# Perceiver block on one core: most transposes of the feed-forward's activations go from the matrix engine to VectorE squares and an exchange through DRAM

## The chip, the cores and the metric

One Trainium2 chip, of which one core is used. The metric is the device time of one execution in microseconds (us), lower is better. The engines of the core are named as in the profile: PE (TensorE, matrix products; PEld is its weight load), DVE (VectorE), ACT (ScalarE), POOL (GpSimd), SP (SyncE, which here only issues DMAs).

## The reference

A perceiver block in float32: cross-attention of 16 x 64 latents to 16 contexts of 512 rows, a differential self-attention, and a feed-forward with blockwise FP4 rounding. Each is added to the residual `x`. Only the feed-forward is touched by the change:

```python
x = x + _L0_xattn_ref(ctx_1024, _layernorm(x), ...)        # 16 batches x 64 latents, width 512
x = x + _L0_attn_ref(_layernorm(x), ...)
x = x + _L0_ffn_ref(_layernorm(x), w_gate, w_up, w_down)   # hidden width 1408

def fp4_quant_dequant(x):          # blocks of 16 along the last axis
    scale = max(|block|) / 6       # at least 1e-12
    return nearest of {0, .5, 1, 1.5, 2, 3, 4, 6} to |x| / scale, times sign(x) * scale

def fp4_linear(x, w):
    return einsum('bsk,nk->bsn', fp4_quant_dequant(x), fp4_quant_dequant(w))

def ffn(x):
    h = silu(fp4_linear(x, w_gate)) * fp4_linear(x, w_up)
    return fp4_linear(h, w_down)
```

## The kernel before

The 1,024 latent rows are eight tiles of 128 rows (`t` = 0 to 7). The kernel runs the latents' projections, cross-attention, self-attention and the feed-forward one after the other; the start of the feed-forward is woven into the end of self-attention. The order that each engine follows up to there is written out by hand and pinned by `in_order()`. What `FeedForward.rest` issues after that is put in order, engine by engine, by the framework's own planner, which works with a simulated timeline; the engines then run their queues strictly in that order and meet through semaphores.

Every float32 product is made of three products of rounded halves: an operand `a` is split into `hi`, a copy in the reduced format fp32r, and `lo = a - hi`, and `terms` (L114) runs hi by hi, hi by lo and lo by hi. So the first operand's upper half is needed for the first two thirds of a product and its lower half for the last third.

The feed-forward is a list of 24 steps `(t, c)`, where `c` is a chunk of the hidden width: 512, 512 and 384 columns. The list starts (0,0), (0,1), (1,0), (1,1), (0,2), (1,2), and goes on tile by tile with (2,0), (2,1), (2,2) up to (7,2). Step `n` (`step`, L1820) issues:

- `gate` and `up` of step n: 12 matmuls each, left operand the transposed activations `x` of the tile (`fx`, both halves), into a pair of PSUM banks `gu` of which there are two;
- between them `turn_h` of step n-2: three or four PE transposes of 128 x 128 (`ht`, L171) into PSUM, the upper half copied by ACT (`hh`, L129), the lower half subtracted by DVE (`hl`, L130; it reads `ht` in PSUM and `hh` in SBUF);
- `hidden` of step n: ACT's silu of the gate bank (L1744), DVE's product with the up bank (L1745), and the FP4 rounding of `h` (`fp4_steps`, L194 to L210). All of the rounding is on DVE but one ACT operation in the middle (L205), which stands between DVE's L202 and L207;
- `down` of step n-3: 12 or 9 matmuls on `hh` and `hl`; after chunk 2 DVE adds the residual (L1797) and SP stores the tile `y`;
- where a tile's turn has come, `norm` of a later tile (layer norm and FP4 rounding of x in `fz`; here the two broadcast products L199 and L210 are POOL's), and `turn` (four PE transposes `xt`, ACT's copy, DVE's subtraction `fx`).

Of the kernel before, what the change touches and what calls it, by code (L numbers as in the profile page):

```python
# [9 lines left out]
F32 = mybir.dt.float32  # L10
F32R = mybir.dt.float32r
# [3 lines left out]
ALU = mybir.AluOpType  # L15
# [4 lines left out]
P = 128  # L20
D = 512
KC = D // P
# [7 lines left out]
CHUNKS = [(at, min(D, FF - at)) for at in range(0, FF, D)]  # L30
# [15 lines left out]
def f32(t):  # L46

    return t.bitcast(F32)


class Common:
# [7 lines left out]
    def __init__(self, ctx, tc):  # L59
        nc = tc.nc  # L60
        self.tc, self.nc = tc, nc
        const = ctx.enter_context(tc.tile_pool(name="const", bufs=1))
        self.const = const
        self.ident = const.tile([P, P], F32, tag="ident", name="ident")
        make_identity(nc, self.ident)
        self.mhalf = const.tile([P, 8], F32, tag="mhalf", name="mhalf")
        nc.gpsimd.memset(self.mhalf, -0.5)
        self.mmagic = const.tile([P, 1], F32, tag="mmagic", name="mmagic")
        nc.gpsimd.memset(self.mmagic, -MAGIC)
        self.masked = const.tile([P, 1], F32, tag="masked", name="masked")  # L70
        nc.gpsimd.memset(self.masked, -MASKED)
        self.rsw, self.rsT = (const.tile([P, 32], F32, tag=n, name=n) for n in ("rsw", "rsT"))
        nc.gpsimd.memset(self.rsw, 0.0)
        self.x_mv = const.tile([P, NT, 3], F32, tag="x_mv", name="x_mv")
        self.x = [const.tile([P, D], F32, tag=f"x{t}", name=f"x{t}") for t in range(NT)]
        self.small = ctx.enter_context(tc.tile_pool(name="small", bufs=4))
        self.slots = ctx.enter_context(tc.tile_pool(name="slots", bufs=1))
        self.ps_mm = ctx.enter_context(tc.tile_pool(name="ps_mm", bufs=3, space=PSUM))
        self.ps_sim = ctx.enter_context(tc.tile_pool(name="ps_sim", bufs=2, space=PSUM))
        self.ps_av = ctx.enter_context(tc.tile_pool(name="ps_av", bufs=1, space=PSUM))  # L80
# [137 lines left out]
class Scratch:  # L218


    def __init__(self, ctx, tc):
        pool = ctx.enter_context(tc.tile_pool(name="scratch", bufs=1, space=DRAM))

        def dram(name, shape):
            return pool.tile(shape, F32, tag=name, name=name)


        self.q = [dram(f"q_d{g}", [P, KC, GT * P]) for g in range(NT // GT)]
        self.k = [dram(f"k_d{g}", [P, KC, GT * P]) for g in range(NT // GT)]
        self.v = [dram(f"v_d{p}", [P, D]) for p in range(NT)]  # L230
        self.rs = [dram(f"rs_d{b}", [1, N]) for b in range(B)]

        self.gu = {
            (w, c): dram(f"{w}_d{c}", [P, 2, KC, n])
            for w in ("g", "u")
            for c, (_, n) in enumerate(CHUNKS)
        }
        self.dn = [dram(f"d_d{c}", [P, 2, n // P, D]) for c, (_, n) in enumerate(CHUNKS)]


class Quantise:
# [129 lines left out]
class CrossWeights:  # L371
# [20 lines left out]
    def turn(self):  # L392
        cm, nc = self.cm, self.cm.nc
        n = len(self.NAMES) * KC
        pt = cm.tr("vec_t")[:, :n]
        nc.tensor.transpose(pt, self.rows, cm.ident[:n, :n])
        nc.scalar.copy(self.vec, pt)
# [73 lines left out]
def _latents(ctx, tc, cm, sc, i, cw, cx, sa):  # L471
# [373 lines left out]
    def turned(*tiles):  # L845
        for p in tiles:
            turn(p)
            upper(p)
            lower(p)
# [10 lines left out]
def cross_attention(tc, cm, sc, i, cw, cx, w1, w2, att, quant):  # L860
# [276 lines left out]
    for b in range(B):  # L1137
# [16 lines left out]
        if b:  # L1154
            turn(b - 1)
            turn_latents(b - 1)
# [88 lines left out]
        quant.tick()  # L1245
        cx.load(b + 3)
    turn(B - 1)
    turn_latents(B - 1)
    att.product(0, "Wq")
# [35 lines left out]
def by_half(t):  # L1285

    return t.rearrange("p (c h) d -> p h c d", h=2)


class SelfAttention:  # L1290
# [199 lines left out]
    def squares(self, t):  # L1490
        o = self.st["o", t] = self.w1.tile([P, 8, S], F32, tag="oh", name=f"on_{t}")
        for h, po in enumerate(self.st["po", t]):
            self.nc.scalar.activation(by_half(o)[:, h], po, AF.Square)
# [146 lines left out]
class FeedForward:  # L1640


    def __init__(self, tc, cm, sc, w1, w2, out):
        self.tc, self.cm, self.nc, self.sc, self.out = tc, cm, tc.nc, sc, out
        self.w1, self.w2 = w1, w2
        self.W, self.st = {}, {}

        self.steps = [(t, c) for t in range(2) for c in range(2)] + [(t, 2) for t in range(2)]
        self.steps += [(t, c) for t in range(2, NT) for c in range(len(CHUNKS))]

    def weights(self, *names):

        at = {
            ("g", 0): (4, 5),
            ("u", 0): (10, 11),
            ("d", 0): (6, 7),
            ("g", 1): (0, 1),  # L1660
            ("u", 1): (8, 9),
            ("d", 1): (4 * ["prT"], ["o", "o", "q_hl"]),
            ("g", 2): (["four1", "four2"], 4 * ["v"]),
            ("u", 2): (2, 3),
            ("d", 2): (["pr", "oh"], ["pr", "q_e"]),
        }
        bufs = {"prT": 4, "v": 4, "o": 2, "pr": 2}
        for w, c in names:
            src = self.sc.dn[c] if w == "d" else self.sc.gu[w, c]
            _, _, nk, n = src.shape  # L1670
            for h, home in enumerate(at[w, c]):
                chunks = self.W[w, c, h] = []
                if isinstance(home, int):
                    pieces = [(self.cm.slot(home, f"{w}T{c}{h}", F32R, (P, nk, n)), nk)]
                else:
                    pieces = []
                    for x, tag in enumerate(home):
                        many = 2 if tag in ("four1", "four2", "q_hl", "pr") else 1
                        t = self.w1.tile(
                            [P, many, n], F32R, tag=tag, bufs=bufs.get(tag, 1), name=f"{w}T{c}{h}_{x}"  # L1680
                        )
                        pieces.append((t, many))
                for t, many in pieces:
                    k = len(chunks)
                    self.nc.sync.dma_start(f32(t), src[:, h, k : k + many])
                    chunks += [t[:, x, :] for x in range(many)]

    def norm(self, t):
        for step in self.norm_steps(t):
            step()  # L1690

    def norm_steps(self, t):
# [11 lines left out]

        return [begin, norm] + 5 * [lambda: next(st["fp4", t])]

    def turn(self, t):
        cm, w2 = self.cm, self.w2
        pt = cm.ps_av.tile([P, D], F32, tag="av", name=f"xt_{t}") if t < 2 else cm.tr(f"xt_{t}")
        cm.transpose_chunks(pt, self.st.pop(("z", t)), KC)  # L1710
        both = w2.tile([P, 2, KC, P], F32R, tag=f"fx{t % 2}", name=f"fx_{t}")
        cm.split(both[:, 0], both[:, 1], pt.rearrange("p (k n) -> p k n", n=P))
        self.st["x", t] = both[:, 0], both[:, 1]
# [38 lines left out]
    def turn_h(self, s):  # L1752
        cm, w2 = self.cm, self.w2
        t, c = s
        n = CHUNKS[c][1]
        nk = n // P
        pt = cm.tr(f"ht_{t}_{c}")
        cm.transpose_chunks(pt, self.st.pop(("h", s)), nk)
        hh = w2.tile([P, KC, P], F32R, tag="two_h", bufs=2, name=f"hh_{t}_{c}")[:, :nk, :]
        hl = w2.tile([P, KC, P], F32R, tag="two_l", bufs=2, name=f"hl_{t}_{c}")[:, :nk, :]  # L1760
        src = pt[:, :n].rearrange("p (k n) -> p k n", n=P)
        if s == self.steps[-1]:
            for k in range(nk):
                cm.nc.scalar.copy(hh[:, k, :], src[:, k, :])
            cm.nc.vector.tensor_tensor(hl, src, f32(hh), ALU.subtract)
        else:
            cm.split(hh, hl, src)
        self.st["hT", s] = hh, hl

    def down(self, s):  # L1770
        cm, nc = self.cm, self.nc
# [48 lines left out]
    def step(self, n):  # L1820
        s = self.steps[n] if n < len(self.steps) else None
        if s:
            self.gate(s)
        if 0 <= n - 2 < len(self.steps):
            self.turn_h(self.steps[n - 2])
        if s:
            self.up(s)
            self.hidden(s)
            if s[1] == 2 and 2 <= s[0] < NT - 2:
                self.norm(s[0] + 2)  # L1830
            elif s in ((1, 1), (0, 2)):
                self.norm(1 + s[1])
        if 0 <= n - 3:
            self.down(self.steps[n - 3])
        if s and (s == (1, 2) or (s[1] == 1 and 2 <= s[0] < NT - 1)):
            self.turn(s[0] + 1)
# [103 lines left out]
```

## Time and profile before

| | |
|---|---|
| time, median of 3 runs | 882.5 us (882.25 to 883.4) |
| the profiled execution: its own time, its span | 882.59 us, 880.8 us |
| busy, share of the span: PE, DVE, ACT, POOL | 99%, 78%, 45%, 35% |
| granted PE clock | 1.00 |
| PE transposes `ht`, in groups of 3 or 4 | 88, from 696.2 to 874.3 us |
| PE transposes `xt` | 32, from 667.2 to 837.4 us |
| first `gu` matmuls of chunk 2 of tile 3, 4, 5, 6, 7 | 764.85, 789.15, 813.48, 837.80, 861.69 us |
| DMA share of the 16 engines, 716 to 862 us | 0.01 to 0.06 |

The page gives one execution. A row of the timeline has the start in us, the duration in us, the engine, the source line, the operation, the tiles written and read, the shape and the count; brackets at its end give the engine's idle time before it and what ended it. Successive DVE operations can overlap by some hundredths of a microsecond, so their pace is read from start to start. The table of stretches gives the busy time of PE, PEld, DVE, ACT and POOL in each stretch, then the PE clock, the DMA share and GB/s.

### The profile page before, as it was taken

The numbers are of one execution on the slowest core, as the hardware profiler recorded it, in microseconds if no ns is written. First come the engines' busy times: TensorE is split into PE (matmuls) and PEld (weight loads), VectorE is DVE, ScalarE is ACT, GpSimd is POOL, SyncE is SP. The second block draws the span as 40 slices with busy tenths as digits, with TensorE's granted clock in tenths as the row PEclk, the third lists the DMA queues.
The fourth block names the chain that finished last, engine by engine and source line by source line (L and its number), as shares of the span: only waits on it lengthen the run. The fifth ranks groups of instructions, "written<-read, shape, count | busy, mean of one in ns | idle before, by whom it ended". The sixth has DMA issues, their size and how long they took to land.

```text
span 880.8 us, 17489 instructions
## 1 busy us (share of the span) xinstructions
PE 873.1 (99%) x6743; PEld 719.2 (82%) x6743; DVE 685.2 (78%) x1425; ACT 398.2 (45%) x787; POOL 305.3 (35%) x357
## 2 busy tenths in 40 slices
PE   8999999999999999999999999999999999999998
PEld 8988777877787888778877887888888888888887
DVE  7734457788788786787878866588998897888876
ACT  5653454544554535354436455555555233332221
POOL 2344334335353352352543622545543120111100
PEclk9999999999999999999999999999999999999999
DMA  8464554644555455435644361240007330000000
GB/s 295 148 234 171 163 163 143 201 144 146 187 175 154 142 163 167 135 112 179 185 131 146 123 197 56 91 192 2 1 3 312 143 144 13 13 13 13 12 13 25
DMA packets 80379, 111.12 MB, mean 126 GB/s; under 512 B 33176, under 2 KB 39080, under 8 KB 79016
## 3 DMA queue, kind: packets, MB, share of 16 engines
q1 hardware_dynamic: 80136, 109.48, 37.9%
q8 instruction: 53, 0.87, 0.4%
q0 software_dynamic: 160, 0.52, 0.2%
q14 instruction: 30, 0.25, 0.1%
HBM read 84.26 MB, written 25.72 MB: 125 GB/s over the span
## 4 chain that ended last, share of the span: by engine, by line
PE 94%; DVE 4%; POOL 1%; issue 0%; ACT 0%; DMA 0%; DVEq 0%; ACTq 0%; POOLq 0%
PE pv L121 20%; PE pk L121 20%; PE gu L121 14%; PE dn L121 7%; PE av L1043 5%; PE sim L971 4%; PE lv L121 2%; PE po L121 2%; PE Wv L121 2%; PE wo L121 2%; PE prt L1008 2%; PE Wq L121 2%; PE lq L121 2%; PE lk L121 2%; PE Wk L121 2%; PE ht L171 1%
## 5 line engine op out<-in xcount | busy, mean ns | idle before, releaser
L121 PE MATMUL pv<-xvh,x 128*128 128x512 f32 x512 | 132.7, 393 | 0.0
L121 PE MATMUL pk<-x,xkh 128*128 128x512 f32 x512 | 128.2, 392 | 0.0
L121 PEld LDWEIGHTS pv<-xvh,x 128*128 128x128 f32 x512 | 94.8, 188 | 26.0 <-issue 7.0
L121 PEld LDWEIGHTS pk<-x,xkh 128*128 128x128 f32 x512 | 94.9, 188 | 19.5 <-issue 0.4
L994 ACT ACTIVATE pr<-pr,least 128x576 f32<-128x576 f32 x64 | 49.2, 770 | 60.8 <-DVE least L990 60.8
L945 DVE TENSOR_TENSOR k<-pk,row 128x512 f32<-128x512 f32 x64 | 43.2, 675 | 40.2 <-PE pk L121 39.4
L368 POOL TENSOR_TENSOR x<-raw,x 128x512 fp32r<-128x512 f32 x32 | 41.3, 1289 | 84.6 <-ACT x L362 73.0
L958 ACT ACTIVATE v<-pv,rs 128x512 f32<-128x512 f32 x64 | 43.2, 684 | 59.8 <-PE pv L121 59.6
L121 PE MATMUL pv<-xvl,x 128*128 128x512 f32 x256 | 68.5, 389 | 0.0
L121 PE MATMUL pk<-x,xkl 128*128 128x512 f32 x256 | 68.5, 389 | 0.0
L121 PE MATMUL gu<-uT,fx 128*128 128x512 f32 (+1 forms) x288 | 66.7, 377 | 0.0
L121 PE MATMUL gu<-gT,fx 128*128 128x512 f32 (+1 forms) x288 | 65.8, 376 | 0.0
L121 PEld LDWEIGHTS gu<-gT,fx 128*128 128x128 f32 x288 | 52.2, 188 | 7.6 <-ACT fx L129 0.2
L121 PEld LDWEIGHTS gu<-uT,fx 128*128 128x128 f32 x288 | 51.9, 188 | 7.2
L121 PEld LDWEIGHTS pv<-xvl,x 128*128 128x128 f32 x256 | 48.0, 188 | 10.2
L121 PEld LDWEIGHTS pk<-x,xkl 128*128 128x128 f32 x256 | 48.0, 188 | 10.1
L990 DVE CUSTOM_DVE_ANT_0 pr<-sim,mask 128x576 f32<-128x576 f32 x64 | 45.9, 754 | 6.9 <-PE sim L971 6.6
L205 ACT ACTIVATE qe_h<-qe_h,mmagic 128x512 f32<-128x512 f32 (+1 forms) x24 | 16.5, 688 | 66.4 <-DVE qe_h L202 64.3
L321 DVE BATCH_NORM_STATS2 cst<-nat 128x6 f32<-128x512 f32 x64 | 42.8, 669 | 3.6 <-DMA nat<-in_ctx_dram 3.6
L121 PE MATMUL dn<-dT,hh 128*128 128x512 f32 x170 | 42.9, 392 | 0.0
L1043 PEld LDWEIGHTS av<-v,prT 128*64 128x64 f32 x1024 | 36.7, 138 | 6.9 <-issue 5.7
L1043 PE MATMUL av<-v,prT 128*64 128x64 f32 x1024 | 40.8, 224 | 0.0
(348 smaller groups left out, 1906.6 us busy)
## 6 DMA issues: line engine op xcount, KB each, us to landing
nat<-in_ctx_dram SPq DMA_DIRECT2D x16, 1024.0 KB
raw<-in_ctxT_dram SPq DMA_DIRECT2D x64, 256.0 KB
d_d<-qhl_d SPq DMA_DIRECT2D x11, 512.0 KB
row<-rs_d SPq DMA_DIRECT2D x16, 256.0 KB
g_d<-qhl_g SPq DMA_DIRECT2D x8, 512.0 KB
u_d<-qhl_u SPq DMA_DIRECT2D x8, 512.0 KB
gT<-g_d SPq DMA_DIRECT2D x4, 1024.0 KB
uT<-u_d SPq DMA_DIRECT2D x4, 1024.0 KB
```

The costliest lines, as they stand in the source:

```text
L121: self.nc.tensor.matmul(ps, lhsT=p[i], rhs=p[j], start=start and n == 0, stop=stop and n == last)
L171: self.nc.tensor.transpose(pt[:, c * P : (c + 1) * P], src[:, c * P : (c + 1) * P], self.ident)
L205: nc.scalar.activation(e, e, AF.Relu, bias=self.mmagic, scale=MAGIC)
L321: nc.vector.bn_stats(st, self.nat[b][:, j, :])
L368: by.tensor_tensor(lo, self.raw[:, c, :], f32(hi), ALU.subtract)
L945: nc.vector.tensor_tensor(k[:, S : S + N], ps, cx.row[b], ALU.mult)
L958: nc.scalar.mul(v, ps, cx.rs[b][:, t : t + 1])
L971: nc.tensor.matmul(pss[r][c * S : (c + 1) * S, h, :half], lhsT=queries[b % 2][rows, m, :], rhs=st["k"][m][rows, at : at + half], start=Tru ...
L990: nc.vector.tensor_tensor_reduce(two(pr), ps[:, :, :half], two(mask), -1.0, BIG, ALU.add, ALU.min, least)
L994: nc.scalar.activation(pr, pr, AF.Exp, bias=least, scale=-1.0, accum_out=st["tot"][:, t : t + 1])
L1008: nc.tensor.transpose(pt[:, c, at : at + S], state[b]["pr", a][rows, r, first + j * P : first + (j + 1) * P], cm.ident[rows, rows],)
L1043: nc.tensor.matmul(st["av"][rows, 2 * a + r, :], lhsT=w[:, rows], rhs=v[:, at : at + S], start=(n == 0), stop=(n == len(pairs) - 1),)
```

## The change

Two kinds of transposes leave PE: those of x for the tiles 2 to 7, and those of h for the steps (1,1) to (7,0) of the list, 19 of 24. In their place:

- `squares`: one DVE transpose of 32 x 32 squares (all squares of a tile in one instruction, the four groups of 32 columns brought forward as the outer index), then four DMAs on SP, one for each group of 32 partitions, that write 512-byte (or 384-byte) runs to a DRAM buffer `sq`, of which there are four;
- `regroup`: one DMA on SP that reads the buffer back with the groups exchanged (`raw`), ACT's copy of the upper half from `raw`, and POOL's subtraction of the lower half.

`send` and `send_h` issue the first part right after the rounding, `turn` and `turn_h` the second at their old place in the step. The SBUF tiles `k0`, `k1`, `k2` and `four0`, used by the attention before, hold the squares and `raw`, two each in turn. x of the tiles 0 and 1, h of the first three steps and of the last two keep PE, and there the lower half stays with DVE.

```diff
@@ Scratch
+        self.sq = [dram(f"sq_d{n}", [4, 32, 4, KC * 32]) for n in range(4)]
@@ FeedForward.__init__
+        self.far = self.near = 0
+        self.far_steps = self.steps[3:-2]
@@ FeedForward
+    def squares(self, src, nk, name):
+        nc = self.nc
+        tag = ("k0", "k1")[self.far % 2]
+        t = self.w1.tile([P, 4, KC * 32], F32, tag=tag, name=f"sq_{name}")[:, :, : nk * 32]
+        nc.vector.transpose(
+            t.rearrange("p q (k l) -> p q k l", l=32),
+            src.rearrange("p (k q l) -> p q k l", q=4, l=32),
+        )
+        far = self.sc.sq[self.far % len(self.sc.sq)][:, :, :, : nk * 32]
+        self.far += 1
+        for n in range(4):
+            nc.sync.dma_start(far[:, :, n].rearrange("q f r -> f q r"), t[n * 32 : (n + 1) * 32])
+        return far
+
+    def regroup(self, hi, lo, far, nk, name):
+        nc = self.nc
+        pool, tag = ((self.w1, "k2"), (self.w2, "four0"))[self.near % 2]
+        self.near += 1
+        raw = pool.tile([P, 4, KC * 32], F32, tag=tag, name=f"sr_{name}")[:, :, : nk * 32]
+        nc.sync.dma_start(raw, far.rearrange("q f t r -> (q f) t r"))
+        src = raw.rearrange("p t (k l) -> p k t l", l=32)
+        hi, lo = (x.rearrange("p k (t l) -> p k t l", l=32) for x in (hi, lo))
+        nc.scalar.copy(hi, src)
+        nc.gpsimd.tensor_tensor(lo, src, f32(hi), ALU.subtract)
+
+    def send(self, t):
+        if t >= 2:
+            self.st["zs", t] = self.squares(self.st.pop(("z", t)), KC, f"x_{t}")
+
+    def send_h(self, s):
+        if s in self.far_steps:
+            self.st["hs", s] = self.squares(self.st.pop(("h", s)), CHUNKS[s[1]][1] // P, f"h_{s[0]}_{s[1]}")
@@ turn
-        pt = cm.ps_av.tile([P, D], F32, tag="av", name=f"xt_{t}") if t < 2 else cm.tr(f"xt_{t}")
+        if t >= 2:
+            both = w2.tile([P, 2, KC, P], F32R, tag=f"fx{t % 2}", name=f"fx_{t}")
+            self.regroup(both[:, 0], both[:, 1], self.st.pop(("zs", t)), KC, f"x_{t}")
+            self.st["x", t] = both[:, 0], both[:, 1]
+            return
+        pt = cm.ps_av.tile([P, D], F32, tag="av", name=f"xt_{t}")
@@ turn_h
+        if s in self.far_steps:
+            self.regroup(hh, hl, self.st.pop(("hs", s)), nk, f"h_{t}_{c}")
+            return
         pt = cm.tr(f"ht_{t}_{c}")
         cm.transpose_chunks(pt, self.st.pop(("h", s)), nk)
@@ step
             self.hidden(s)
+            self.send_h(s)
             if s[1] == 2 and 2 <= s[0] < NT - 2:
                 self.norm(s[0] + 2)
+                self.send(s[0] + 2)
             elif s in ((1, 1), (0, 2)):
                 self.norm(1 + s[1])
+                self.send(1 + s[1])
```

More of the change, by code (lines that the diff above doesn't have):

```diff
@@ L1756, in turn_h @@
         nk = n // P
+        hh = w2.tile([P, KC, P], F32R, tag="two_h", bufs=2, name=f"hh_{t}_{c}")[:, :nk, :]
+        hl = w2.tile([P, KC, P], F32R, tag="two_l", bufs=2, name=f"hl_{t}_{c}")[:, :nk, :]
+        self.st["hT", s] = hh, hl
+        if s in self.far_steps:
+            self.regroup(hh, hl, self.st.pop(("hs", s)), nk, f"h_{t}_{c}")
+            return
         pt = cm.tr(f"ht_{t}_{c}")
         cm.transpose_chunks(pt, self.st.pop(("h", s)), nk)
-        hh = w2.tile([P, KC, P], F32R, tag="two_h", bufs=2, name=f"hh_{t}_{c}")[:, :nk, :]
-        hl = w2.tile([P, KC, P], F32R, tag="two_l", bufs=2, name=f"hl_{t}_{c}")[:, :nk, :]
         src = pt[:, :n].rearrange("p (k n) -> p k n", n=P)
@@ L1767, in turn_h @@
             cm.split(hh, hl, src)
-        self.st["hT", s] = hh, hl
     def down(self, s):
```

## The prediction

> **What bounds the kernel now.** I read the page first: PE is busy for the whole span at full clock, and DVE, on average, is not.
>
> ```profile
> PE 873.1 (99%) x6743; PEld 719.2 (82%) x6743; DVE 685.2 (78%) x1425; ACT 398.2 (45%) x787; POOL 305.3 (35%) x357
> ```
>
> The averages mix stages, so next the stretches, cut where chunk 2 of tiles 4, 5 and 6 begins (columns: PE, PEld, DVE, ACT, POOL, clock, DMA share, GB/s):
>
> ```profile
> 789.15:813.48 24.33, 24.33 (x122) 20.88 (x121) 20.98 (x43) 7.29 (x12) 2.22 (x2) 1.00 0.03 12
> 813.48:837.80 24.32, 24.32 (x121) 20.86 (x121) 20.97 (x43) 6.56 (x11) 2.22 (x2) 1.00 0.03 11
> 837.80:861.69 23.89, 23.89 (x118) 20.50 (x117) 17.27 (x35) 6.00 (x10) 0.00 (x0) 1.00 0.03 12
> ```
>
> One tile takes 24.3 us of PE without a gap. DVE is busy for 21.0 of them in the first two rows, which also prepare x of a later tile, and 17.3 in the third, which doesn't. The timeline shows what DVE does in the other 3.3:
>
> ```profile
> 821.77 0.49 DVE L199 TENSOR_TENSOR h<-h,qm_h 128x384 f32<-128x384 f32 x1
> 822.30 1.10 DVE L202 TENSOR_SCALAR qe_h<-h 128x384 uint32<-128x384 uint32 x1
> 824.14 0.56 DVE L207 SCALAR_TENSOR_TENSOR h<-qe_h,h 128x384 f32<-128x384 f32 x1 [0.74 <-ACT qe_h L205]
> ...
> 830.02 1.25 DVE L199 TENSOR_TENSOR h<-h,qm_h 128x512 f32<-128x512 f32 x1
> ...
> 835.31 0.69 DVE L1745 TENSOR_TENSOR h<-gu,h 128x512 f32<-128x512 f32 x1 [0.23 <-ACT h L1744]
> ```
>
> It waits 0.74 to 0.85 for ACT between L202 and L207, three times a tile, and only 0.23 us for a product of PE. So DVE's own queue, waits included, fills about 23.9 of 24.3 us: it is the next limit, 2% behind PE. L202 on 384 columns takes 0.36 at 728.80 but 1.10 here, and L199 1.25 instead of 0.69: in both a POOL operation runs:
>
> ```profile
> 822.03 1.16 POOL L199 TENSOR_TENSOR fz<-fz,qm_x 128x512 f32<-128x512 f32 x1 [15.62 <-DVE qm_x L197]
> 829.65 1.07 POOL L210 TENSOR_TENSOR fz<-fz,qs_x 128x512 f32<-128x512 f32 x1 [6.47 <-DVE qm_h L196]
> ```
>
> DVE's operation ends some 0.2 to 0.55 after POOL's, as if it had begun when POOL was done.
>
> **What leaves PE.** 93 transposes: 12 groups of four and 7 of three for h, 6 of four for x. From weight load to weight load a group of four costs 0.50 to 0.56 and one of three 0.45:
>
> ```profile
> 790.93 0.53 PEld L171 LDWEIGHTS ht<-ident,h 128*128 128x128 f32 x4
> 791.43 2.04 PEld L121 LDWEIGHTS gu<-uT,fx 128*128 128x128 f32 x12
> ```
>
> 18 x 0.53 + 7 x 0.45 = 12.7 us, all of it on the path now. A tile would take PE 24.3 - 2.0 = 22.3.
>
> Here a rule speaks against the change. The Trainium skill, "VectorE: DVE Perf Modes", section "The three transpose paths", advises TensorE for a 128 x 128 transpose into PSUM and VectorE only for 32 x 32, and lists 390 against 311 ns for one in bf16. This trace has 0.13 per fp32 transpose in the stream of weight loads; by the page's 390 ns the removed work would be an estimated 36 us.
>
> **What DVE gets.** It loses the subtractions (0.69 at 512 columns, 0.55 at 384) and gets as many square transposes, which the weights' rounding already uses:
>
> ```profile
> L287 DVE STREAM_TRANSPOSE qhl_u<-qw_u x12: 537/694/715, 184.8 to 406.5; 128x512 f32<-128x512 f32 x8, 128x384 f32<-128x384 f32 x4
> ```
>
> Busy time is even. The order changes, though, and I walked the changed program's DVE queue for one tile (42 instructions, from L207 of chunk 0 to the next) with start-to-start spacings of the tile above: 0.61 between independent 512-column operations, 0.72 when one needs the other, 0.47 at 384, 0.2 to 0.4 in the small chain L195 to L197, 1.28 (384: 1.10) from L202 to L207 where nothing stands between. Chunk 1's part gives 6.4, chunk 2's 7.1, chunk 0's and x's 7.8: 21.3 us. Against 24.3, that is 1.3 less for POOL's two blockages, put back below, 0.4 for waits that came from PE, 0.85 for one wait on L205 that x's transpose now fills, 1.4 for dependent neighbours that move apart; and 0.9 more because x's transpose waits for POOL's L210 at the end of its rounding, with DVE's queue behind it (the next L207) standing still.
>
> **What POOL gets.** Four subtractions a tile of a form that the trace has in cross-attention, where both inputs are in SBUF too:
>
> ```profile
> L368 POOL TENSOR_TENSOR x<-raw,x x32: 1268/1286/1304, 75.6 to 510.2; 128x512 fp32r<-128x512 f32 x32
> ```
>
> POOL has room (2.2 of 24.3). But while it subtracts, DVE's L195, L196, L199, L202, L207, L208 and L210, which read two SBUF tiles or are short scalar operations, may stand still; its products with PSUM and its reductions ran on beside L368. The bounds are 0 and 1.29 each. Going by where the four fall in the queue (exchange time below), x's costs 1.0, chunk 0's 0.45, chunk 1's 1.0 and chunk 2's nothing: 2.5 a tile. With the 0.73 of POOL's L199 and 0.4 for the four landings that each transpose must see before it reuses its buffer (waits of 0.02 to 0.05), DVE's period is 21.3 + 2.5 + 0.7 + 0.4 = **24.9 us** a tile.
>
> The Trainium skill, "SBUF — State Buffer", section "Who interferes with whom", calls the port that both engines share an exclusive lock for the whole instruction, taken by whoever begins first. The rows agree on the direction; if every subtraction cost its whole 1.29, as the rule allows at worst, the period would be an estimated 27.6 and the kernel an estimated 10.8 us slower than forecast here.
>
> **The exchange.** An isolated store of a tile `y` is issued in 0.33 and its last semaphore comes 1.9 to 2.0 after the issue; an isolated 256 KB load (`raw<-in_ctxT`) takes 2.2 to 2.5. Four issues of 0.33 with their waits: the fourth begins 1.25 after the transpose, lands 1.5 later, the load 2.4 after that: 5.2 us. ACT's upper copy is 0.62, POOL's lower 1.29. A chunk's halves are then ready about 18.5 and 19.8 us after its `up`; PE wants them one tile later, at 22.3 (and 1.8 more for the lower). So there is a lead of about 3 us, for x too, and no wait while DVE keeps pace. SP queues the stores of `y` and the next squares behind the load's wait, but has one exchange per 6 to 8 us.
>
> **Where it is not hidden.** x of tile 2 has no lead:
>
> ```profile
> 718.88 0.69 DVE L208 SCALAR_TENSOR_TENSOR fz<-fz,qe_x 128x512 f32<-128x512 f32 x1
> ...
> 719.65 1.06 POOL L210 TENSOR_TENSOR fz<-fz,qs_x 128x512 f32<-128x512 f32 x1 [3.14 <-DVE qm_x L196]
> ...
> 726.14 3.84 PE L121 MATMUL gu<-gT,fx 128*128 128x512 f32 x16
> ```
>
> Rounded at 720.7, transposed at 721.4, back at 726.6, copied at 727.3 or, behind other ACT work, 727.6. PE, by then 1.1 ahead, would want it at 725.1: 2.5 us lost.
>
> **The sum.** While x of tiles 4 to 7 is prepared, four periods, DVE loses 24.9 - 22.3 = 2.6 a tile against PE: 10.4, of which the lead takes 3.0, so PE waits 7.4. In the last two tiles DVE, without x, catches up and PE sets the end. 12.7 - 2.5 - 7.4 = 2.8 us gained. The profiled execution took 882.6 (span 880.8 and 1.8 around it; median 882.5): 882.6 - 2.8 = **879.8 us**.
>
> **Rivals.** (a) DVE keeps pace: POOL's subtractions fall into waits that DVE has anyway (it sits idle 0.8 twice a tile), and the period is under 22.9. For it: of the 32 subtractions L368 in the trace, 19 delayed DVE by under 0.03 us. Against: DVE was less full there. The gain is 12.7 - 2.5, less up to 2: 872.4 to 874. (b) Slower: ACT's queue. The copies that wait for a landing stand ahead of L205 of the next rounding (chunk 1's copy ahead of x's L205, x's copy ahead of chunk 1's), and DVE waits for L205. Each microsecond by which an exchange exceeds 5.2 costs about 1 per tile in four tiles, 1 of the lead and 1 at tile 2: 6 in all. It decides from 5.7 us on, where the gain is gone; at 7 us it gives 879.8 + 10.8 = 890.6. For it: SP's issues take 0.5 to 0.6 when queues are full, as around 240 us. Against: the queues are at 0.01 to 0.06 here. (c) POOL subtracts more slowly on strided tiles (its L1457, strided, averages 1.54): 0.25 more, four a tile, four tiles, is 4 us: 883.8, no change.
>
> **Numbers.** The forecast (DVE sets the pace, with (c) within it, 876 to 884) has 0.43, (a) 0.20, (b) 0.37. What this kernel's measurement can tell from no change is 0.2%, 880.7 to 884.3. Of the forecast 0.25 lie below, 0.13 within, 0.05 above: faster 0.45, same 0.13, slower 0.42. The range leaves out half of (a), below 872.5, and the worst of (b), above 891; the forecast's own range is 876 to 884.
>
> **What would show it.** Right: no `ht` between 717 and 868, a first gap of PE of 2 to 3 us near 726 behind ACT's `fx`; from about 770 to 840 gaps of PE behind ACT's `hh` or POOL's `hl`, tiles of about 24.9, then of 22.4; DVE's L195, L207 or L210 stretched while POOL subtracts. Wrong: tiles of 22.3 throughout (then DVE had more room than I count), or DVE waiting long for L205 with ACT idle behind a landing (then it is the exchange), or a granted clock below 1.00.

## The result, and the profile after

The changed kernel takes 891.15 us (median of 5 runs, 890.82 to 892.42) against 882.3 us for the kernel before on the same chip (881.83 to 883.4): a ratio of 1.0104, interval 1.0092 to 1.0116. The forecast was 879.8, with a range from 872.5 to 891. The profiled execution has a span of 890.0 us, 9.2 more than before. In what follows L1734 and L1735 are ACT's upper copy and POOL's lower half in `regroup`, L1715 the square transpose, L1722 and L1731 the stores and the load, L1787 silu, L1788 the product for h.

The busy line of the page: PE has 93 transposes less, and yet the span is longer.

```profile
PE 867.9 (98%) x6650; PEld 712.5 (80%) x6650; DVE 691.8 (78%) x1425; ACT 397.2 (45%) x787; POOL 338.6 (38%) x382
```

What PE waited for in the feed-forward (waiting engine and tile, releaser, us in total, times, longest):

```profile
PE gu L121 <- ACT fx L1734: 8.1, 4, 2.5
PE ht L171 <- DVE h L210: 4.4, 1, 4.4
PE dn L121 <- ACT hh L1734: 2.1, 1, 2.1
```

The first row is x, which comes late four times; h's copy is late once, at tile 2; the second row is one wait in the last tile. From then on h has in fact the lead that the prediction gave it, and x has none.

One exchange of x, in the timeline of the changed kernel (tile 6's x):

```profile
813.87 0.71 DVE L1715 STREAM_TRANSPOSE sq_x<-fz 128x512 f32<-128x512 f32 x1 [0.95 <-POOL fz L210]
814.61 1.77 SPq L1722 DMA_DIRECT2D sq_d<-sq_x  x4
817.79 0.34 SPq L1731 DMA_DIRECT2D sr_x<-sq_d  x1
820.48 0.62 ACT L1734 CAST fx<-sr_x 128x512 fp32r<-128x512 f32 x1 [4.93 <-DMA sr_x<-sq_d]
821.15 4.60 PE L121 MATMUL gu<-gT,fx 128*128 128x512 f32 x12 [2.50 <-ACT fx L1734]
```

From the end of the transpose (814.58) to the copy it takes 5.9 us; 5.2 were predicted. The four issues take 1.77 (0.44 each, not 0.33). PE stands still 2.50 us, and then needs 4.60 for twelve matmuls that take 2.88 elsewhere: its clock. Stretches of the changed kernel around that wait and in the last tile (start and end, length, busy time of PE, PEld, DVE, ACT, POOL, clock, DMA share, GB/s):

```profile
797.60:799.60 2.00, 2.00 (x10) 1.68 (x9) 2.00 (x5) 0.06 (x1) 0.00 (x0) 1.00 0.44 139
822.60:824.00 1.40, 1.40 (x4) 1.09 (x4) 1.40 (x4) 0.00 (x0) 0.00 (x0) 0.50 0.36 64
877.50:879.00 1.50, 1.50 (x5) 1.21 (x4) 0.98 (x3) 0.36 (x1) 0.00 (x0) 0.50 0.00 0
```

The granted clock halves for 3.4 us after the wait of 2.50 and for 5.1 after that of 4.43; after waits of 2.06 (at 795.64) and 1.88 (at 847.54) it stays at 1.00. The length of the wait alone doesn't decide it, for in run 3 below a wait of 1.84 us halves the clock as well (0.50 from 866.1 to 869.0; eight `dn` matmuls take 3.52 instead of 1.98):

```profile
865.57 0.88 PE L171 MATMUL ht<-ident,h 128*128 128x128 f32 x4 [1.84 <-DVE h L210]
866.10 3.52 PE L121 MATMUL dn<-dT,hh 128*128 128x512 f32 x8
```

The Trainium skill, "TensorE: Matmul & The Clock Gate", section "Part 1: The HAM clock gate", gives these two ratios, half and full, and says that an idle window of about 3.4 us brings the lower one. The ratio agrees; here waits of 2.50 and 1.84 us were enough.

POOL's subtraction and the DVE operation beside it:

```profile
815.63 1.01 POOL L1735 TENSOR_TENSOR hl<-sr_h,hh 128x384 fp32r<-128x384 f32 x1 [1.80 <-ACT hh L1734]
815.67 1.52 DVE L208 SCALAR_TENSOR_TENSOR h<-h,qe_h 128x512 f32<-128x512 f32 x1
821.17 1.29 POOL L1735 TENSOR_TENSOR fx<-sr_x,fx 128x512 fp32r<-128x512 f32 x1 [4.53 <-ACT fx L1734]
821.75 1.25 DVE L207 SCALAR_TENSOR_TENSOR h<-qe_h,h 128x512 f32<-128x512 f32 x1 [0.99 <-ACT qe_h L205]
```

L208 and L207 take 0.69 by themselves; here they end 0.5 us after POOL. And L207 waited 0.99 for L205 instead of 0.85, because ACT's copy of `fx` stood ahead of L205.

The last tile, where DVE's order and ACT's meet:

```profile
872.28 0.62 ACT L1734 CAST hh<-sr_h 128x512 fp32r<-128x512 f32 x1 [1.54 <-DMA sr_h<-sq_d]
872.80 0.48 ACT L1787 ACTIVATE h<-gu 128x384 f32<-128x384 f32 x1
873.32 0.56 DVE L1788 TENSOR_TENSOR h<-gu,h 128x384 f32<-128x384 f32 x1 [1.13 <-ACT h L1787]
873.79 0.99 DVE L210 TENSOR_TENSOR h<-h,qs_h 128x512 f32<-128x512 f32 x1
874.84 1.12 PE L171 MATMUL ht<-ident,h 128*128 128x128 f32 x4 [4.43 <-DVE h L210]
```

A landing holds ACT's copy, silu stands behind the copy, DVE's product behind silu, L210 behind the product, and PE behind L210. The four transposes of this group take 1.12 instead of 0.53: the clock again.

**A second account.** The following stretches run from the end of h's rounding in step (2,2) to the end of that in (7,2), five tiles, in the kernel before and in the changed one:

```profile
755.70:873.93 118.23, 118.23 (x584) 101.50 (x583) 98.35 (x197) 32.92 (x55) 8.03 (x7) 1.00 0.03 12
```

```profile
757.45:881.03 123.58, 112.71 (x504) 94.91 (x503) 104.05 (x196) 32.04 (x55) 34.24 (x26) 0.96 0.31 85
```

The span's 9.2 us are 1.75 at the start of this stretch (tile 2), 5.35 in it and 2.1 after it (9.0 from the last rounding to the end, 6.9 before). PE is busy for the whole 118.2 before and has 10.9 to spare after; DVE is busy for 104.05 and idle for 19.5. Of this idle time 12.5 are waits for ACT's L205 in the middle of DVE's own roundings, and none is a wait for a gate or up product of PE (the 1.1 behind silu at 873.32 goes back to a landing, as shown above). So it is DVE's queue that takes 123.6 us.

### The profile page after: what moved, and what is told of

Its sections match the earlier page's. It is cut to its first block, busy times and chain, and to the rows that moved or that the text cites. A ratio compares the mean times of both kernels' runs of the same rounds, so it can differ in the third digit from the quotient of the medians.

```text
span 890.0 us, 17554 instructions
## 1 busy us (share of the span) xinstructions
PE 867.9 (98%) x6650; PEld 712.5 (80%) x6650; DVE 691.8 (78%) x1425; ACT 397.2 (45%) x787; POOL 338.6 (38%) x382
## 4 chain that ended last, share of the span: by engine, by line
PE 74%; DVE 12%; DMA 6%; ACT 2%; SPq 2%; issue 2%; POOL 2%; DVEq 0%; ACTq 0%; POOLq 0%
PE pv L121 20%; PE pk L121 20%; PE av L1044 4%; PE sim L972 4%; PE gu L121 2%; PE lv L121 2%; PE po L121 2%; DMA sr_h<-sq_d 2%; PE Wv L121 2%; PE prt L1009 2%; PE Wq L121 2%; PE lq L121 2%; PE lk L121 2%; PE wo L121 2%; PE Wk L121 2%
## 5 line engine op out<-in xcount | busy, mean ns | idle before, releaser
L121 PEld LDWEIGHTS pk<-x,xkh 128*128 128x128 f32 x512 | 94.9, 188 | 19.5 <-issue 0.4
L121 PE MATMUL gu<-gT,fx 128*128 128x512 f32 (+1 forms) x288 | 67.7, 382 | 8.1 <-ACT fx L1734 8.1
L121 PE MATMUL gu<-uT,fx 128*128 128x512 f32 (+1 forms) x288 | 64.0, 371 | 0.0
L1735 POOL TENSOR_TENSOR hl<-sr_h,hh 128x512 fp32r<-128x512 f32 (+1 forms) x19 | 25.0, 1317 | 72.7 <-ACT hh L1734 72.7
L121 PE MATMUL dn<-dT,hh 128*128 128x512 f32 x170 | 44.8, 405 | 2.1 <-ACT hh L1734 2.1
L205 ACT ACTIVATE qe_h<-qe_h,mmagic 128x512 f32<-128x512 f32 (+1 forms) x24 | 16.5, 686 | 54.8 <-DVE qe_h L202 54.8
```

Of the source, the lines that this page charges most:

```text
L121: self.nc.tensor.matmul(ps, lhsT=p[i], rhs=p[j], start=start and n == 0, stop=stop and n == last)
L205: nc.scalar.activation(e, e, AF.Relu, bias=self.mmagic, scale=MAGIC)
L1735: nc.gpsimd.tensor_tensor(lo, src, f32(hi), ALU.subtract)
```

## The experiments

Theories: **E**, the exchange is too long, x has no lead and ACT's other work stands behind landings; **P**, POOL's subtractions hold DVE up (the shared port of the prediction) and DVE sets the pace; **T**, the loss is in the last tile's order alone. After the first four runs P and E merged into **D**: DVE sets the time up to its last rounding, and both POOL's subtractions and the landings lengthen its queue. Each run was measured beside the kernel before, which took 882.2 to 882.5 us each time; differences from the changed kernel's 891.15 are between sessions.

**1. No trip through DRAM.**

```diff
@@ squares
-        for n in range(4):
-            nc.sync.dma_start(far[:, :, n].rearrange("q f r -> f q r"), t[n * 32 : (n + 1) * 32])
-        return far
+        return t
@@ regroup
-        nc.sync.dma_start(raw, far.rearrange("q f t r -> (q f) t r"))
-        src = raw.rearrange("p t (k l) -> p k t l", l=32)
+        src = far.rearrange("p t (k l) -> p k t l", l=32)
```

> Leaves out the trip through DRAM: ACT and POOL read the squares where VectorE wrote them (four SBUF buffers instead of two and two), so the groups of partitions are not exchanged and the values are not the reference's; all instructions of DVE, ACT, POOL and PE stay. Theory E (the exchange is too long: x, and behind it ACT's other work, comes late): the waits of PE for fx (8.1 us in four) and the 4.4 us wait in the last tile go, the clock stays at 1.00, tiles take 22.3 to 22.9, time 871 to 876. Theory P (POOL's subtractions hold DVE up, so DVE sets the pace at 24.9 a tile): DVE is as slow as before, tiles stay at 24.5 or more while x is prepared, time 880 to 886. Theory T (the loss is mostly in the last tile, where DVE's order puts a product ahead of h's rounding): little change up to 864 us, the end still 26 us after the last chunk 2 begins, time 884 to 890.

Measured: 883.2 us against 882.4 before (ratio 1.0009, 1.0000 to 1.0018), in P's range. Up to 828 us PE runs freely at 22.6 a tile, as E said; chunk 2 of tile 7 begins at 852.05, 9.6 us earlier than in the kernel before. All of it is given back at the end, 8.0 us in one wait (PE's timeline) and most of the rest at the halved clock behind it:

```profile
866.45 1.11 PE L171 MATMUL ht<-ident,h 128*128 128x128 f32 x4 [7.97 <-DVE h L210]
```

PE had merely run ahead of DVE: the time from the end of an `up` product to DVE's use of it grows from 1.7 us in step (2,2) to 8.9 in (7,2). In the stretch from rounding to rounding:

```profile
755.90:872.65 116.75, 107.60 (x490) 91.80 (x489) 103.03 (x194) 31.82 (x54) 32.51 (x25) 0.96 0.03 12
```

DVE's busy time hardly changes (103.0 for 104.05), its idle time falls from 19.5 to 13.7. That is what the trip costs DVE.

**2. No lower halves.**

```diff
@@ regroup
-        nc.gpsimd.tensor_tensor(lo, src, f32(hi), ALU.subtract)
@@ turn / turn_h
-            self.st["x", t] = both[:, 0], both[:, 1]
+            self.st["x", t] = both[:, 0], both[:, 0]
+            self.st["hT", s] = hh, hh
```

> Leaves out POOL's subtractions for everything that goes by squares; the products take the upper half in place of the lower one, so PE does the same matmuls on other values. The trip through DRAM stays. Theory E: the landings are as late as before, PE waits for fx about 8 us in all and 4.4 in the last tile: 887 to 892. Theory P: DVE gets 2.5 us a tile back in four to five tiles, its period falls to 22.4, the waits go: 876 to 881. Theory T: 887 to 891.

Measured: 880.38 us (ratio 0.9979, 0.9969 to 0.9988), in P's range. PE's waits for fx fall from 8.1 to 2.2 us although the trip is as long as ever, and the one in the last tile from 4.4 to 1.0: DVE hands x over earlier. The same stretch:

```profile
757.49:870.71 113.22, 110.46 (x514) 93.91 (x512) 90.99 (x195) 32.30 (x55) 8.51 (x7) 1.00 0.34 91
```

DVE's busy time falls by 13.1 us, that is 0.69 for each of POOL's 19 subtractions in it. Idle rises by 2.7, for DVE now waits for others a little more.

**3. Only h by squares.**

```diff
-        if t >= 2:
+        if False:        # turn and send: x of all tiles stays on PE
```

> Only h goes by squares; x of all tiles is transposed on PE again, with ACT's copy and DVE's subtraction. PE gets 6 x 0.53 = 3.2 us of work back. Theory E with x as the part that has no lead: the 8.1 us of waits for fx go and with them the dip of the clock to 0.94 (about 1.6 us): 891.2 + 3.2 - 9.7 = 884.7, range 882 to 886, the end of the last tile unchanged. If h is late too: 888 to 892. Theory P: three subtractions a tile instead of four, about 1 us less a tile: 887 to 891.

Measured: 880.54 us (ratio 0.9974, 0.9964 to 0.9983), below every number given. The waits for fx are gone but for 0.7, the clock is 1.00 in the steady tiles, and the wait in the last tile is 1.8. From rounding to rounding DVE is busy for 101.4 us and idle for 15.8 (104.05 and 19.5 with x): E priced only PE's waits for x, and x had cost DVE's queue 6 us as well.

**4 and 5. x one step earlier.**

```diff
-            if s[1] == 2 and 2 <= s[0] < NT - 2:
+            if s[1] == 1 and 2 <= s[0] < NT - 2:
@@ second version only
-        self.sq = [dram(f"sq_d{n}", [4, 32, 4, KC * 32]) for n in range(4)]
+        self.sq = [dram(f"sq_d{n}", [4, 32, 4, KC * 32]) for n in range(8)]
```

> The rounding of x, its square transpose and its stores are issued one step (about 8 us) earlier for the tiles 4 to 7, nothing else is changed; the planner orders each engine anew. Theory E with x's missing lead: three to four waits for fx of 1.9 to 2.5 us go, the clock is 1.00 in the steady tiles: 891.2 - 6.4 - 1.6 = 883, range 881 to 885. Theory P: DVE has the same work, its pace stays, PE waits elsewhere (hh, hl) for about the same time: 888 to 892. Theory T: the last tile keeps its 6.8 us loss in either case.

939.45 us, and not the test that it was meant to be: with x a step earlier five exchanges are under way, and with four DRAM buffers x of a tile is read from the buffer after x of the next tile was stored there. So the values are wrong, and the read waits for a later tile's rounding (PE waits 25.4 us for fx). The second version has eight buffers:

> The rounding of x, its square transpose and its stores are issued one step (about 8 us) earlier for the tiles 4 to 7; there are eight DRAM buffers instead of four, since more exchanges are under way. Rival E (x's missing lead is the loss): three to four of the waits of PE for fx go, clock 1.00 in the steady tiles, 881 to 885. Theory D: PE's waits for fx go, but DVE has the same work and the same stalls; its last rounding ends at about the same time (880 to 881 us of the span) and so does the kernel: 888 to 892.

Measured: 887.34 us (ratio 1.0057, 1.0039 to 1.0076), 0.7 under D's range and above E's. What PE waits for now:

```profile
PE dn L121 <- ACT hh L1734: 6.9, 7, 1.9
PE ht L171 <- DVE h L210: 3.4, 1, 3.4
```

After tile 2 no wait for fx is left (6.4 us in the changed kernel); waits for h, 4.9 us, are there in its place (all 6.9 less one of 1.9 in tile 2). DVE's last rounding ends at 877.7 instead of 881.0. So x's missing lead was the place where the delay was seen, and only 3.8 us of the 8.9.

**6. Neither trip nor lower halves** (the edits of 1 and 2 together).

> Leaves out both the trip through DRAM and POOL's subtractions (values are not the reference's); PE, ACT and DVE keep every instruction. Theory D (formed on the runs before this one: DVE sets the time to the end; its own pace with x is 25.4 us a tile in the changed kernel, of which POOL's port takes 2.1 and the stalls of ACT behind landings 1.3): the two parts add, DVE's period falls to 22.0 and below PE's 22.3, PE sets the end, 871 to 875. If the two parts overlap (the same stall counted twice): 877 to 880. Theory T (a loss in the last tile alone, by the order of DVE's queue): 880 to 884.

Measured: 871.3 us (ratio 0.9874, 0.9859 to 0.9889), the low end of D. The two parts add: 8.0 and 10.8 alone, 19.9 together.

```profile
827.89:850.48 22.59, 22.59 (x107) 19.39 (x105) 18.05 (x39) 5.51 (x9) 0.00 (x0) 1.00 0.03 13
```

PE is busy for the whole of each tile, and DVE uses the `up` product 0.56 us after its end in (2,2), (5,2) and (7,2) alike. Only here does nearly all that left PE become a gain: 11.1 us of the 12.7, where run 2 gained 2.0 and run 1 nothing.

**7. A longer exchange.**

```diff
-            nc.sync.dma_start(far[:, :, n].rearrange("q f r -> f q r"), t[n * 32 : (n + 1) * 32])
+            for q in range(0, 4, 2):
+                nc.sync.dma_start(far[q : q + 2, :, n].rearrange("q f r -> f q r"),
+                                  t[n * 32 : (n + 1) * 32, q : q + 2])
```

> Each of the four stores of an exchange is cut in two, eight DMA issues instead of four: by the 0.44 us that an issue takes, the exchange gets 1.76 us longer, nothing else. The prediction's price (about 6 us of time for each microsecond of the exchange) gives 891.2 + 10.6 = 901.8. Theory D prices it by the run without the trip: 8.0 us for an exchange of 5.9, that is 1.35 us for each microsecond, so 891.2 + 2.4 = 893.6, up to 896. If the exchange were hidden: 891.

915.69 us (ratio 1.0373, 1.0357 to 1.0388): far above both prices, 24.5 us for 1.76. SP's queue shows why:

```profile
782.08 3.60 SPq L1723 DMA_DIRECT2D sq_d<-sq_x  x8
785.78 9.16 SPq L1723 DMA_DIRECT2D sq_d<-sq_h  x16
795.05 0.37 SPq L1734 DMA_DIRECT2D sr_x<-sq_d  x1
```

In the planner's new order the sixteen stores of two chunks of h stand between the stores of x and the load that brings it back, and SP issues in order: x's load begins 13.0 us after its first store (3.2 in the changed kernel). PE waits 12.3 us for it. So this run does not price a microsecond of the exchange; it shows what happens when issue time fills SP's queue.

**8. The lower halves on DVE.**

```diff
-        nc.gpsimd.tensor_tensor(lo, src, f32(hi), ALU.subtract)
+        nc.vector.tensor_tensor(lo, src, f32(hi), ALU.subtract)
```

> The lower halves of what goes by squares are subtracted by DVE, from SBUF, instead of POOL; nothing else is changed. Theory D: DVE gets 25 subtractions of 0.55 to 0.69 (16.6 us), and loses the time that it stood still beside POOL's 25 (14.6 us by the trace of the changed kernel): 891.2 + 2 = 893, range 890 to 896. If POOL's port were not what slows DVE: 891.2 + 16.6 less some cover, 900 to 908. If DVE were not the bound: 880 to 885.

Measured: 886.6 us (ratio 1.0040, 1.0026 to 1.0054), 3.4 under D's range and 4.5 faster than the change itself. From rounding to rounding:

```profile
760.02:876.10 116.08, 110.62 (x506) 93.55 (x505) 100.43 (x214) 33.16 (x55) 7.95 (x7) 0.99 0.32 88
```

Against run 2 (90.99) the 19 subtractions take DVE 9.4 us, 0.50 each. A subtraction on POOL took 0.69 of DVE's time; DVE does it in less.

**9 to 12. Parts of the change.** x alone (`far_steps = []`); and, each with the edit of 3, h alone up to tile 5, h of chunks 0 and 2 up to tile 5, h of chunk 2 alone:

```diff
-        self.far_steps = self.steps[3:-2]
+        self.far_steps = self.steps[3:-6]                              # h alone, near the end on PE
+        self.far_steps = [s for s in self.steps[3:-6] if s[1] in (0, 2)]  # two chunks
+        self.far_steps = [s for s in self.steps[3:-2] if s[1] in (2,)]    # one chunk
```

> Only x goes by squares (tiles 2 to 7); h of all steps is transposed on PE. PE loses 6 x 0.53 = 3.2 us. Theory D: DVE has one POOL subtraction (0.58) more in each tile that prepares x, and stands behind x's landing once: about 24.3 to 24.6 a tile, as long as PE's 23.8 plus waits; with no square transposes of h in its queue it still keeps pace better than with h: 881 to 884. Theory E (x's trip has no lead, whatever DVE does): PE waits 1.9 to 2.5 us for fx at four tiles: 886 to 890.

> As the run with h alone by squares, and the steps from (6,0) on keep PE too: PE gets about 2 us back in tiles 6 and 7, where it ran 4 to 6 us ahead of DVE; DVE loses POOL's port and the waits for landings there. Theory D: DVE's pace in the last two tiles falls from 22.2 to about 21.6, so 880.5 - 1.2 = 879.3, range 878 to 880.5. If PE sets the end: 881 to 883.

> h of chunks 0 and 2 goes by squares up to tile 5, the rest and x stay on PE: two exchanges a tile instead of four. Theory D: PE's tile is 24.33 - 0.98 = 23.35, DVE stands beside two POOL subtractions a tile (1.2 us); the two are about even: 879 to 881. If more on PE is always worse: 881 to 882.

> Only h of chunk 2 (384 columns) goes by squares, in all tiles. Theory D: PE's tile is 24.33 - 0.45 = 23.88, DVE stands beside one POOL subtraction a tile (0.6): PE still sets the pace, 7 groups x 0.45 = 3.1 us less: 879.3, range 878.5 to 881. If the exchange of even one chunk costs DVE more than PE gains: 882 to 884.

Measured: x alone 882.93 (ratio 1.0007, 0.9999 to 1.0016), no gain and no loss, as D said; h with the end on PE 880.21 (0.9972, 0.9961 to 0.9983), in D's range; two chunks 878.09 (0.9950, 0.9938 to 0.9963), 0.9 better than D's range; one chunk 880.23 (0.9976, 0.9966 to 0.9985), in D's range. The two-chunk version beats both kernels by most, of those that leave nothing out. Its stretch in a steady tile:

```profile
785.91:809.41 23.50, 23.50 (x117) 20.17 (x115) 20.78 (x43) 7.04 (x12) 4.92 (x5) 1.00 0.18 51
```

PE is busy throughout, 0.8 us a tile less than before, and DVE (20.8 busy) still keeps up: a mean of 0.39 us of DVE's time lost beside each of POOL's ten subtractions (by how much DVE's operations beside them are stretched), and no wait of PE in the feed-forward but the 0.4 in the last product.

## Why the prediction was wrong

**The step that failed** is the one after the sum of waits: "In the last two tiles DVE, without x, catches up and PE sets the end." DVE didn't catch up. The end is DVE's last rounding and what follows it. By the prediction's own periods, four with x and one without in these five tiles, but with DVE to the end, the span is 757.45 + 4 x 24.9 + 22.4 + 6.9 = 886.35 (the start as measured); it said 878.0. These 8.35 us are most of the miss of 12.0. The mistake was to let a lead of PE count as time: run 1 has that lead, 9.6 us of it, and hands back all of it.

**Terms that were mis-sized.** The five periods of DVE, from the end of the rounding of one chunk 2 to the next, are 25.44, 25.41, 25.51, 24.47 and 22.75 us. x is still in the fourth of them: x of tile 7 is transposed at 840.32 and subtracted at 847.56, and the roundings of (6,2) and (7,2) end with these L210.

```profile
840.32 0.71 DVE L1715 STREAM_TRANSPOSE sq_x<-fz 128x512 f32<-128x512 f32 x1 [0.95 <-DMA sr_h<-sq_d]
847.56 1.29 POOL L1735 TENSOR_TENSOR fx<-sr_x,fx 128x512 fp32r<-128x512 f32 x1 [5.07 <-ACT fx L1734]
857.73 0.55 DVE L210 TENSOR_TENSOR h<-h,qs_h 128x384 f32<-128x384 f32 x1
880.47 0.56 DVE L210 TENSOR_TENSOR h<-h,qs_h 128x384 f32<-128x384 f32 x1
```

So DVE's period with x, 24.9, measured 25.21 in the mean of four, 1.2 in all; without x, taken as no more than 22.4, it measured 22.75, 0.35 more. The end after the last rounding, 6.9, measured 9.0, because PE, at half clock from 874.84 to 879.9, is still behind with its products when the rounding ends (DVE waits 2.35 us for them, 0.45 before); no term stood for the clock. 8.35 + 1.2 + 0.35 + 2.1 is the 12.0.

**Terms that held.** PE's work per tile, 22.3: 22.6 in run 6. POOL's blockage, 2.5 a tile: 13.1 over five tiles, one of them without x. The loss at tile 2, 2.5 us near 726, held roughly: PE waited 2.08 and 1.65 at 722 to 729, the first time for a copy of h, which the prediction had not seen, and DVE is 1.75 later at (2,2). "Busy time is even": without POOL's share DVE was even 7.4 us less busy than before (98.35 and 90.99), so the square transpose itself is no burden.

**The rule and the row.** The prediction weighed the whole-instruction lock of the Trainium skill, "SBUF — State Buffer", section "Who interferes with whom", against the traces of L368. Over 19 subtractions of 1.0 to 1.7 us DVE lost 0.69 each: DVE does stand still beside them, and the mean price is half of a subtraction's length, close to the 0.62 that the prediction's 2.5 for four amounts to.

**The rivals.** (a), DVE keeping pace, priced that case rightly, and run 6 reaches it (871.3 for 872.4 to 874), but only with POOL's and the trip's share both taken out; its reason, that POOL's subtractions fall into waits that DVE has anyway, is not so. (b) had the right mechanism in part and the wrong price: the exchange is 5.9 us, past the break-even of 5.7, for which (b) gives 879.8 + 0.7 x 6 = 884.0. The copies waiting on landings ahead of L205, as it described, are there (0.99 and 1.53 us for L207 at 821.75 and 848.14 instead of 0.85), but the trip's price of 8.0 us, measured by run 1, is less than the lower halves' 10.8. The lead "for x too" wasn't there: the square transpose of tile 6's x ends at 814.58, PE wants the copy at 818.65, and the way there takes 6.5 us. PE waited 1.65 to 2.5 us for four of its six copies. Run 5 shows that this decides where PE waits and less than half of how long.

**What would show it.** Of the signs given, no `ht` between 717 and 868, the early loss and the stretched L195, L207 and L210 came true; PE's gaps after tile 2 stood behind `fx`, not `hh` or `hl`; and the clock fell below 1.00, which the text had named as a sign against itself.

How much of the trip's cost comes through x's landing, and how much through h's, is not separated: the runs with one of the two also change POOL's share. The planner orders every run anew, so each price above has the change of order in it; no run holds the order fixed. Why the planner put the stores of run 7 in that order stays open.

## What to carry to other kernels

When two engines are within a few per cent of each other, write both queues down to their last instruction: an engine that runs ahead has gained nothing until the other's last result is in. Take a helper engine's price on the engine that it holds up, not on itself: here a subtraction on an idle POOL cost DVE 0.69 us, more than the 0.50 of DVE doing it. And move only as much as the next limit can bear: two of the four exchanges a tile gave 0.5%, all four lost 1%.

## What the runs showed of the hardware

- PE's clock fell to 0.50 after waits of 2.50 and 4.43 us and didn't after 1.88 and 2.06; but in run 3 it fell after 1.84, and in run 5 after 1.94 (at 724.01). The length of a wait alone didn't decide.
- A store of 32 partitions by four 512-byte runs takes 0.44 us to issue on SP, a load of the whole tile 0.34.
- Beside POOL's subtractions DVE's square transposes kept their 0.71 us (run 7, at 800.73, the whole of it beside one; in the changed kernel none falls beside one), while in the changed kernel an L195 on 24 elements a partition (at 852.05) took 1.27 instead of 0.17.
